# A list schedule at the head of a scan kernel in place of one at its tail

## The chip, the cores and the metric

The kernel runs on one core of a Trainium2 chip. The metric is device time in microseconds (us), the median of several runs. A core has TensorE (PE, matrix products; PEld is its loading of weights), VectorE (DVE), ScalarE (ACT), GpSimd (POOL) and SyncE (SP, which here only issues transfers). Each engine executes its own instructions strictly in the order of the program and waits for the others through semaphores. So the order in which the program emits the work decides what an engine does while it could do something else.

## What is computed

Four images of 64 x 64 pixels with 96 channels go through two layers. Cut to what matters:

```python
x = x + L0(_gn(x))            # _gn: group norm, 32 groups of 3 channels
t = tokens(x)                 # 4 images x 4096 tokens x 96
t = t + attn(_ln_t(t))        # linear attention: no softmax
t = t + ffn(_ln_t(t))         # 96 -> 384 -> 96, products in 8-bit, sums in 16-bit floats

def L0(x):                    # a selective scan over the 4096 tokens
    proj = layernorm(x) @ W_in + b_in
    value, gate, delta = ...  # 96 channels each
    A, B, C = ...             # 96 channels x 16 states each
    h_new = d * (A_t * h) + d * (B_t * u_t)         # token after token
    y = sigmoid(gate) * sum(C_t * h_new, states)
    return y @ W_out + b_out
```

The attention has no softmax. So it is a 97 x 96 matrix R for each image, made from the Gram matrix of all normalised tokens of the image: no token's attention can begin until the last chunk of its image has been scanned.

## The kernel before

An image is cut into 8 chunks of 512 tokens (`TC`), so there are 32 chunks. In each, the 96 x 16 = 1536 channel states are 12 tiles (`NT`) of 128 rows: 4 groups of states (`sh`) times 3 groups of 32 channels (`cg`). One step of the main loop is one tile; there are `K` = 384 steps. A tile is made so:

```python
def b_copy(self):   # ACT: bu <- B product + bias
    nc.scalar.activation(self.bu, self.b_ps, AF.Identity, bias=self.bias(0))
def b_mul(self):    # POOL: times delta*u, replicated over partitions
    nc.gpsimd.tensor_tensor(self.bu, self.bu, rep[self.b, self.i][:, 1, self.cg], ALU.mult)
def a_mul(self):    # DVE: (A product + bias) * delta
    nc.vector.scalar_tensor_tensor(self.a_ps, self.a_ps, self.bias(1),
        rep[self.b, self.i][:, 0, self.cg], ALU.add, ALU.mult)
def scan(self):     # DVE: h[t] = A[t] * h[t-1] + bu[t]
    nc.vector.tensor_tensor_scan(self.h, self.a_ps, self.bu,
        0.0 if self.i == 0 else state[self.sh, self.cg], ALU.mult, ALU.add)
# then C: (C product + bias) * h, on DVE (c_mul) or on ACT and POOL (c_copy, c_mul_pool)
```

Each product is three matrix products (high x high, low x high and so on), since weights and input are split into a high and a low half: `high` rounds the weights on ACT, `low` subtracts on DVE, `split_copies` puts the halves together by DMA. `rep` is delta and delta*u of a chunk, each channel four times over the partitions. For most chunks it goes to DRAM and back (`write`, `read`); for chunk 0:

```python
def copy(self, k, cg, engine):
    t = rep[self.b, self.i][:, k, cg]
    for q in range(4):
        engine.dma_start(t[q * 32 : (q + 1) * 32], self.dd[cg * 32 : (cg + 1) * 32, k])
```

The work ahead of the first scan stands in a fixed order:

```python
for n in range(NCH):                      # group norm of image 0
    q.transpose(n, "AM"[n % 2], "gx"); q.stats(n)
q.aggregate(); q.mean(); q.root(); high_dug(); biases(); q.diagonal(); q.spread(); low_dug()
first, second = Front(0, 0), Front(0, 1)
first.centre(nc.vector); first.scale(nc.vector); first.stats(); first.ln.rstd()
for cg in range(NCG): high(0, cg)         # weights of B, by group of channels
first.apply()
for cg in range(NCG): low(0, cg, nc.vector)
...                                       # A and C likewise, chunk 1 begun
first.proj(2); first.d_out(); first.copy(0, 0, nc.sync)
first.proj(0); first.du_out(); first.copy(1, 0, nc.scalar)
...
```

All other work hangs on steps (`at(step, fn)`): for each chunk a `front` from 22 steps ahead of its scan, a `tail` behind it (sum over states, output product, residual, layer norm, Gram matrix), then `ffn`. The group norm of a later image takes ScalarE's sums of its 8 chunks, each loaded into one buffer (`gx`); image 1 has its own steps:

```python
when = [s0 + SUMS + NT * n for n in range(NCH)]
if b == 1:
    when = [4, 7, 8, 14, 20, 32, 44, 56]
```

What would come behind step K goes into a list instead: each job names its engine, an assumed cost, what it waits for and the buffers it takes, and `Plan.run` emits, time after time, the job that can start first (among near ones that of the lower rank, then that with the longest way to the end). While PE has nothing to do, it runs products whose result nobody uses.

```python
a = job("PE", 0.46, attention, after=[a, b == B - 1 and end.last["r"]], take=[...], free=[...])
a = job("DVE", 0.57, residual, after=[a], free=[f"A:a{nm}"])
a = job("DVE", 1.1, ln.stats, t, after=[a], take=[f"mv:{nm}"])
a = job("POOL", 1.3 if vector else 1.8, ln.rstd, not vector, after=[a])
...
for m in range(NK):
    h = job("PE", 0.24, hidden, m, ...)
    c = job("ACT", 0.57, round_hidden, m, ...)
    r.append(job("DVE", 0.3, relu_vector, m, after=[c]))
a = job("ACT", 1.5, quant, after=r, ...)
a = job("PE", 0.5, project_out, after=[a], ...)
...
end.run(stay_awake)
```

Of the kernel before, what the change touches and what calls it, by code (L numbers as in the profile page):

```python
# [41 lines left out]
XBUFS = 15  # L42


@with_exitstack
def conv_attn_hybrid_kernel(
# [62 lines left out]
    def load_gx(b, i, tag="gx"):  # L109

        t = gxt[b, i] = sb(tag, [P, J, C], F32, f"gx_{b}_{i}")
        nc.sync.dma_start(t, gx_v[b, i])


    for i in range(NCH):
        load_gx(0, i, "x")
# [8 lines left out]
    load_x(0, 0)  # L125
    raw0 = load_raw("cha", 0, A0)
    raws = [load_raw("chb", B0, C * S)]
    load_x(0, 1)
    raws += [load_raw("chb", c0, C * S) for c0 in (A0, C0)]
# [5 lines left out]

    gam = const.tile([C, 1], F32, name="gam")
# [6 lines left out]

    brow = sb("bu", [3 * NCG, 32 * S], F32, "brow")
    for k, c0 in enumerate((B0, A0, C0)):
        nc.scalar.dma_start(
            brow[k * NCG : (k + 1) * NCG, :],
            b_in[c0 : c0 + C * S].rearrange("(g n) -> g n", g=NCG),
        )
# [81 lines left out]
    def split_copies(dst):  # L231
        v = dst.bitcast(F32)
        nc.sync.dma_start(v[0:64, 2], v[0:64, 0])
        nc.sync.dma_start(v[64:P, 2], v[0:64, 1])
# [9 lines left out]
    b_bac = const.tile([P, NSH, 3, NCG], F32, name="b_bac")  # L244

    def cols(k, cg):

        return (
            w_bac[k][:, :, cg].rearrange("k n (s c) -> k n s c", s=S),
            raws[k][:, cg * 32 * S : (cg + 1) * 32 * S].rearrange("k (c s) -> k s c", s=S),  # L250
        )
# [4 lines left out]
    def low_dug():  # L256
        split_low(w_dug, raw0, nc.gpsimd)
        split_copies(w_dug)

    def high(k, cg):  # L260
        dst, src = cols(k, cg)
        nc.scalar.copy(dst[:, 0], src)

    def low(k, cg, engine):
        split_low(*cols(k, cg), engine)
        if cg == NCG - 1:
            split_copies(w_bac[k].rearrange("k n g c -> k n (g c)"))

    def biases():

        row = sb("bu", [3 * NCG, NSH * P], F32, "bias")
        nc.vector.tensor_copy(
            row.rearrange("g (s c) -> g s c", s=S), brow.rearrange("g (c s) -> g s c", s=S)
        )
        ps = bank("M", [P, NSH, 3 * NCG], "bias_ps")
        for sh in range(NSH):
            nc.tensor.transpose(
                ps[:, sh, :], row[:, sh * P : (sh + 1) * P], ident[: 3 * NCG, : 3 * NCG]
            )
        nc.vector.tensor_copy(b_bac.rearrange("p h k g -> p h (k g)"), ps)  # L280
# [29 lines left out]
    class LayerNorm:  # L310
# [13 lines left out]
        def rstd(self, shift=True):  # L324
# [3 lines left out]
            nc.gpsimd.tensor_tensor(self.r, self.r, mhalf, ALU.pow)  # L328
            if not shift:
                return  # L330
            self.nmr = small.tile([P, J], F32, tag="nmr", name=f"nmr_{self.nm}")
            nc.gpsimd.tensor_scalar(self.nmr, self.mv[:, :, 0], -1.0, None, ALU.mult)
            nc.gpsimd.tensor_tensor(self.nmr, self.nmr, self.r, ALU.mult)

# [101 lines left out]
    class GroupNorm:  # L436


        def __init__(self, b):
            self.b = b  # L440
# [9 lines left out]

        def stats(self, n):
            if n == 0:
                self.st = small.tile([C, NCH, 6], F32, tag="gst", name="gst_0", bufs=1)
            nc.vector.bn_stats(self.st[:, n, :], self.ps)
# [49 lines left out]
        def diagonal(self):  # L504
            self.dg = small.tile([C, 2, C], F32, tag="gdg", name=f"gdg_{self.b}", bufs=1)
            for k in range(2):
# [4 lines left out]
        def spread(self):  # L511

            ps = bank("M", [P, 2, C], f"gmr_ps_{self.b}")
            nc.tensor.matmul(
                ps.rearrange("p k c -> p (k c)"), lhsT=ones[0:C, :],
                rhs=self.dg.rearrange("p k c -> p (k c)"), start=True, stop=True,
            )
            t = small.tile([P, 2, C], F32, tag="gmr", name=f"gmr_{self.b}", bufs=2)
            nc.scalar.copy(t, ps)
            gn[self.b] = [t[:, k, :].unsqueeze(1).to_broadcast([P, J, C]) for k in range(2)]  # L520

    def group_norm(b, s0):
# [12 lines left out]
        if b == 1:  # L535
            when = [4, 7, 8, 14, 20, 32, 44, 56]
# [6 lines left out]
        for n, name in ((1, "moments"), (2, "mean"), (4, "root"), (6, "diagonal"), (8, "spread")):  # L543
# [5 lines left out]
    class Front:  # L549
# [3 lines left out]
        def __init__(self, b, i):  # L553
            self.b, self.i, self.nm = b, i, f"{b}_{i}"
            self.ln = LayerNorm(1e-3, f"c_{self.nm}")

# [49 lines left out]
        def copy(self, k, cg, engine):  # L606

            t = rep[self.b, self.i][:, k, cg]
            for q in range(4):
                engine.dma_start(  # L610
                    t[q * 32 : (q + 1) * 32], self.dd[cg * 32 : (cg + 1) * 32, k]
                )
# [18 lines left out]
    def front(b, i, s0, f=None):  # L631
# [10 lines left out]
        at(s + 7, f.transpose)  # L642
        at(s + 8, f.affine)
        at(s + 9, f.upper)
        at(s + 9, f.low)
        at(s + 12, f.proj, 2)
        at(s + 13, f.d_out)
        at(s + 13, f.proj, 0)
        at(s + 14, f.du_out)
        at(s + 14, f.write)  # L650
        at(s + 15, f.read)
# [6 lines left out]
    class Tile:  # L658
# [59 lines left out]
        def slot(self):  # L718
            if self.cg == 0:
# [23 lines left out]
    def state_sum(g, last=None, first=None):  # L743


        if not first:
            y_ps[g] = bank("M" if last is None else "B", [C, TC], f"y_ps_{g}")
        t = chs.pop((g, last or 0))
        for cg in range(NCG):
            nc.tensor.matmul(  # L750
                y_ps[g][cg * 32 : (cg + 1) * 32, :], lhsT=fold, rhs=t[:, cg, :],
                start=not first, stop=(last is None or last == NSH - 1),
                tile_position=(0, 32 * cg), skip_group_check=True,
# [445 lines left out]
```

## Time and profile before

| | us |
|---|---|
| median of 3 runs | 1231.91 (1231.48 to 1232.03) |
| span of the profiled run | 1229.7 |
| first scan starts | 47.00 |
| first scan of the second chunk starts | 90.96 |
| last scan starts | 1152.93 |
| R of the last image done | 1169.2 |
| last GpSimd instruction ends | 1223.4 |

| engine | busy us | share |
|---|---|---|
| PE | 1159.0 | 94% |
| DVE | 1123.9 | 91% |
| POOL | 1028.2 | 84% |
| ACT | 808.4 | 66% |

A timeline line has the start, the duration, the engine, the source line, the operation, output <- inputs, shapes, and in brackets how long the engine had been idle before and what ended that. In a table of stretches the columns are the stretch, its length, the busy time of PE, PEld, DVE, ACT and POOL with counts, the granted TensorE clock (1.00 is full), the share of time in which the DMA engines were busy, and GB/s.

### The profile page before, as it was taken

To read this page: it belongs to the slowest core of one execution; us is meant where nothing else is said; L and a number is where in the kernel's file an instruction comes from. 1 tells how busy PE (TensorE), PEld (TensorE's weight loads), DVE (VectorE), ACT (ScalarE), POOL (GpSimd) and SP (SyncE) were. 2 spreads that over 40 slices of the span, in tenths; PEclk is the share of its full clock that TensorE was granted. 3 is DMA by queue.
4 is the path that set the end of the run, shared out by engine and by line. 5 is a ranking of instruction groups with operands and counts; after the bars stand their busy time and mean duration, and the time that the engine had idled before them with its cause. 6 is when DMAs were issued, how large, how long until landed. Compare 5 with 4: busy or idle time off the path is not lost. (4 is left out here: it accounts for less than half of the span.)

```text
span 1229.7 us, 19138 instructions
## 1 busy us (share of the span) xinstructions
PE 1159.0 (94%) x5866; PEld 872.1 (71%) x5866; DVE 1123.9 (91%) x2095; ACT 808.4 (66%) x1806; POOL 1028.2 (84%) x1168
## 2 busy tenths in 40 slices
PE   3689999999999999999999999999999999999985
PEld 2467777677777777677777777677777777777663
DVE  5479999999999999899999999899999999999884
ACT  3455555555555677677877777777677677777474
POOL 4367888888888888999999889899999899989654
PEclk7789999999999999999999999999999999999999
DMA  8566776677778767777777677677777676767221
GB/s 197 134 136 139 171 163 154 141 155 165 155 172 174 157 149 158 162 154 160 165 175 157 149 169 174 134 155 159 171 156 153 153 173 151 154 149 162 60 70 39
DMA packets 102116, 185.20 MB, mean 151 GB/s; under 512 B 42865, under 2 KB 47413, under 8 KB 102014
## 3 DMA queue, kind: packets, MB, share of 16 engines
q1 hardware_dynamic: 87708, 109.78, 38.0%
q0 software_dynamic: 13536, 73.93, 30.3%
q8 instruction: 46, 0.75, 0.3%
q10 hardware_dynamic: 770, 0.28, 0.1%
q14 instruction: 56, 0.46, 0.1%
HBM read 70.69 MB, written 24.77 MB: 78 GB/s over the span
## 5 line engine op out<-in xcount | busy, mean ns | idle before, releaser
L686 POOL TENSOR_TENSOR bu<-bu,rep 128x512 f32<-128x512 f32 x384 | 559.3, 1504 | 32.9 <-DMA rep<-dd 21.1
L683 ACT ACTIVATE bu<-Bps,b_bac 128x512 f32<-128x512 f32 x384 | 264.2, 688 | 288.2 <-PE Bps L240 275.5
L702 DVE TENSOR_TENSOR_SCAN h<-Aps,state,bu 128x512 f32<-128x512 f32 x336 | 426.4, 1269 | 12.5 <-POOL bu L686 3.5
L695 DVE SCALAR_TENSOR_TENSOR Aps<-Aps,b_bac,rep 128x512 f32<-128x512 f32 x384 | 282.3, 735 | 41.2 <-PE Aps L240 32.8
L240 PE MATMUL Bps<-xs,w 128*128 128x512 f32 x768 | 269.6, 432 | 4.9 <-ACT bu L683 4.8
L240 PE MATMUL Aps<-xs,w 128*128 128x512 f32 x768 | 250.6, 407 | 11.8 <-DVE h L702 10.6
L735 POOL TENSOR_TENSOR ch<-ch,h 128x512 f32<-128x512 f32 x128 | 194.4, 1519 | 2.5 <-ACT ch L732 2.3
L240 PEld LDWEIGHTS Aps<-xs,w 128*128 128x128 f32 x768 | 139.5, 190 | 70.3 <-DVE h L702 41.6
L240 PEld LDWEIGHTS Bps<-xs,w 128*128 128x128 f32 x768 | 130.7, 192 | 46.5 <-issue 26.0
L240 PE MATMUL Bps<-xl,w 128*128 128x512 f32 x384 | 153.1, 399 | 0.0
L240 PE MATMUL Aps<-xl,w 128*128 128x512 f32 x384 | 153.0, 399 | 0.0
L240 PE MATMUL Dps<-xs,w 128*128 128x512 f32 x384 | 121.5, 398 | 0.0
L240 PE MATMUL Cps<-xs,w 128*128 128x512 f32 x384 | 121.0, 396 | 0.0
L741 POOL DMA_DIRECT2D ch<-ch x94 | 88.5, 941 | 20.1 <-DMA ch<-ch 16.5
L726 DVE SCALAR_TENSOR_TENSOR ch<-Dps,b_bac,h 128x512 f32<-128x512 f32 x128 | 94.7, 740 | 0.6 <-PE Dps L240 0.5
L726 DVE SCALAR_TENSOR_TENSOR ch<-Cps,b_bac,h 128x512 f32<-128x512 f32 x128 | 95.0, 742 | 0.0
L240 PEld LDWEIGHTS Bps<-xl,w 128*128 128x128 f32 x384 | 73.0, 190 | 17.3
L240 PEld LDWEIGHTS Dps<-xs,w 128*128 128x128 f32 x384 | 72.6, 189 | 17.9
L240 PEld LDWEIGHTS Cps<-xs,w 128*128 128x128 f32 x384 | 72.2, 188 | 17.9
L240 PEld LDWEIGHTS Aps<-xl,w 128*128 128x128 f32 x384 | 72.4, 189 | 16.9
L240 PE MATMUL Dps<-xl,w 128*128 128x512 f32 x192 | 76.1, 396 | 0.0
L240 PE MATMUL Cps<-xl,w 128*128 128x512 f32 x192 | 75.9, 395 | 0.0
(176 smaller groups left out, 2045.6 us busy)
## 6 DMA issues: line engine op xcount, KB each, us to landing
ch<-ch POOLq DMA_DIRECT2D x94, 768.0 KB, 6.8
rep<-ddd SPq DMA_DIRECT2D x124, 384.0 KB, 7.0
ddd<-dd SPq DMA_DIRECT2D x31, 384.0 KB, 3.1
xl<-lo SPq DMA_DIRECT2D x64, 128.0 KB, 2.9
gx<-in_x_dram SPq DMA_DIRECT2D x32, 192.0 KB, 3.3
x<-in_x_dram SPq DMA_DIRECT2D x32, 192.0 KB, 3.0
xatd<-xat SPq DMA_DIRECT2D x32, 192.0 KB, 3.2
xal<-xatd SPq DMA_DIRECT2D x32, 192.0 KB, 3.9
```

The costliest lines, as they stand in the source:

```text
L240: nc.tensor.matmul(ps, lhsT=wt[:, n], rhs=mv, start=(n == 0), stop=(n == 2))
L683: nc.scalar.activation(self.bu, self.b_ps, AF.Identity, bias=self.bias(0))
L686: nc.gpsimd.tensor_tensor(self.bu, self.bu, rep[self.b, self.i][:, 1, self.cg], ALU.mult)
L695: nc.vector.scalar_tensor_tensor(self.a_ps, self.a_ps, self.bias(1), rep[self.b, self.i][:, 0, self.cg], ALU.add, ALU.mult,)
L702: nc.vector.tensor_tensor_scan(self.h, self.a_ps, self.bu, 0.0 if self.i == 0 else state[self.sh, self.cg], ALU.mult, ALU.add,)
L726: nc.vector.scalar_tensor_tensor(self.slot(), self.c_ps, self.bias(2), self.h, ALU.add, ALU.mult)
L735: nc.gpsimd.tensor_tensor(self.ch, self.ch, self.h, ALU.mult)
L741: nc.gpsimd.dma_start(chs[g, 0], chs.pop((g, sh)), accum_op=ALU.add)
```

## The change

The list schedule moves from the end to the beginning. Up to the sixth step (`START = 6`) all work is emitted by `Plan.run`; behind the last scan the work returns to fixed steps. Four things go with it:

1. Chunk 0 goes without transfers between engines: the low half of its input is subtracted straight into place, and delta and delta*u come already replicated out of TensorE, through weights that hold each column four times (`w_rep`).
2. The weights are split by group of states, in 12 pieces, so that the first steps need only the first pieces.
3. Image 0 is loaded once; its group norm reads the same tiles as the scan path.
4. The sums of image 1's group norm lie seven steps apart.

```diff
     for i in range(NCH):
-        load_gx(0, i, "x")
+        load_x(0, i)
+        gxt[0, i] = xt[0, i]
...
+    def repeat(n):
+        for k, c0 in enumerate((2 * C, 0)):
+            for cg in range(NCG):
+                c = c0 + cg * 32
+                nc.gpsimd.tensor_copy(
+                    w_rep[:, n, k * NCG + cg].rearrange("p (q c) -> p q c", q=4),
+                    w_dug[:, n, c : c + 32].unsqueeze(1).to_broadcast([P, 4, 32]),
+                )
...
-            when = [4, 7, 8, 14, 20, 32, 44, 56]
+            when = [8, 15, 22, 29, 36, 43, 50, 57]
...
-        def copy(self, k, cg, engine):
...
+        def low_in_place(self, n):
...
+            dst, c0, c1 = ((xs[C:P], 64, C), (xl[0:64], 0, 64), (xl[64:P], 0, 64))[n]
+            nc.vector.tensor_tensor(dst, self.ps[c0:c1], xs[c0:c1].bitcast(F32), ALU.subtract)
+        def wide(self, k, cg):
+            ps = self.wd[k, cg] = bank("M", [P, TC], f"wide{k}{cg}_ps")
+            project(ps, w_rep[:, :, k * NCG + cg], split[self.b, self.i])
...
-            end.last["gram"] = job("DVE", 0.25, gram_sum, after=[a], free=[f"B:g{i}"])
...
+        at(s0 + 21, gram)
+        at(s0 + 22, gram_out)
         if i:
+            at(s0 + 23, gram_add)
...
+        if drain:
+            plan = [
+                (-2, fetch), (0, attention), (1, residual), (2, ln.stats, t), (3, ln.rstd),
+                (4, apply), (5, transpose), (5, quant_in),
+                (6, hidden, 0), (6, hidden, 1), (6, hidden, 2),
+                (7, relu, 0), (7, relu, 1), (7, relu, 2), (8, quant),
+                (9, project_out), (9, round_out), (10, bias_out), (11, total), (11, store),
+            ]
...
+    def planned_start():
...
+        hd = job("ACT", 0.43, high_dug, after=[land("raw", 11.9)])
+        ld = job("POOL", 0.8, low_dug, after=[hd])
+        wr = [job("POOL", 2.2, repeat, n, after=[ld]) for n in range(2)]
...
+        a = job("DVE", 0.56, first.scale, nc.vector, after=[c, *g])
+        a = job("DVE", 1.1, first.stats, after=[a])
+        a = job("DVE", 0.07, first.ln.offset, after=[a])
+        a = job("POOL", 1.05, first.ln.root, after=[a])
+        a = job("DVE", 1.3, lambda: first.ln.apply_vector(first.t, first.t), after=[a])
...
+        plan.run(stay_awake)
...
-    end.run(stay_awake)
```

The plan under `drain` is that of the last image, whose chunk i begins at step K + 27 + 2i. With the schedule at the end go its details: the last chunk's sums over states in three parts as the groups come (group 1 added to group 0 by DMA, then 0, 2 and 3 by products; now 1 and 2 are added by DMA first), the last chunk's normalisation on VectorE without the shift, rounding of the output in turn on ACT and DVE (now always DVE for the last image), ReLU by DVE for the chunks of image 2 that are left (now ACT), and the unused products that fill PE. New filler products (128 x 128) stand in the planned start.

## The prediction

> **What bounds the kernel now.** I read the busy shares by slice first, then the busy time of stretches, then the timeline of VectorE around the first scans and behind the last one.
>
> ```profile
> DVE  5479999999999999899999999899999999999884
> PEclk7789999999999999999999999999999999999999
> ```
>
> From the fourth slice (30.7 us each) to the 37th VectorE is full; that middle is 384 steps of one scan each, and the change leaves its work alone. What it touches are the two ends. The busy time of stretches (columns: PE, PEld, DVE, ACT, POOL, clock, DMA share, GB/s) sizes them:
>
> ```profile
> 0.00:47.00 47.00, 21.84 (x75) 15.21 (x76) 21.39 (x48) 20.28 (x33) 16.29 (x37) 0.67 0.76 175
> 47.00:90.96 43.96, 35.68 (x141) 26.48 (x140) 30.02 (x44) 20.85 (x51) 28.15 (x26) 0.88 0.62 139
> 1154.20:1169.20 15.00, 14.07 (x101) 9.70 (x99) 9.69 (x44) 6.28 (x12) 6.55 (x12) 1.00 0.23 67
> 1169.20:1209.00 39.80, 34.28 (x250) 24.02 (x248) 35.64 (x129) 30.09 (x48) 23.54 (x30) 1.00 0.21 61
> ```
>
> Up to the first scan (47.0) no engine is busy half the time: that is latency. The first twelve steps (47.0 to 90.96, chunk 0) leave VectorE idle for 13.9 of 44 us. Behind the last scan (1154.2) it takes 15.0 us until the attention matrix R stands, then VectorE is 90% busy until 1209. Which waits open the start, from the timeline:
>
> ```profile
> 35.61 2.44 SPq L610 DMA_DIRECT2D rep<-dd  x4
> ...
> 40.52 1.27 POOL L686 TENSOR_TENSOR bu<-bu,rep 128x512 f32<-128x512 f32 x1 [10.02 <-DMA rep<-dd]
> ...
> 47.00 1.21 DVE L702 TENSOR_TENSOR_SCAN h<-Aps,bu 128x512 f32<-128x512 f32 x1
> ...
> 55.49 1.22 DVE L702 TENSOR_TENSOR_SCAN h<-Aps,bu 128x512 f32<-128x512 f32 x1 [3.17 <-POOL bu L686]
> ...
> 79.26 1.09 PE L446 MATMUL gx_ps<-ident,gx 128*96 128x128 f32 x4 [4.76 <-DMA gx<-in_x_dram]
> ...
> 90.96 1.27 DVE L702 TENSOR_TENSOR_SCAN h<-Aps,state,bu 128x512 f32<-128x512 f32 x1
> ```
>
> The 24 small copies that spread delta over the partitions hold GpSimd for 10 us, then again before the third scan. At 79 TensorE, in order, stands behind image 1's third load of group-norm input (one buffer; the sums come at steps 4, 7, 8): the tenth scan starts at 75.89, the eleventh at 84.89. And the end:
>
> ```profile
> 1152.93 1.28 DVE L702 TENSOR_TENSOR_SCAN h<-Aps,state,bu 128x512 f32<-128x512 f32 x1
> ...
> 1168.97 0.26 DVE L885 COPY rmat<-r_ps 97x96 f32<-97x96 f32 x1 [0.50 <-PE r_ps L870]
> ...
> 1222.44 0.91 POOL L990 TENSOR_TENSOR o<-x,yb 128x384 f32<-128x384 f32 x1
> ```
>
> **What the Trainium skill says.** (1) "TensorE: Matmul & The Clock Gate", Part 1, What's actually happening: the PE clock runs at half rate after some 3.4 us of idling and at full rate after about as long busy. The trace agrees: granted clock 0.50 from 14 to 32 us, a pair of products 1.22 us at 40.35 against 0.63 at 47.5. (2) "SBUF — State Buffer", Who interferes with whom: a VectorE operation with two SBUF inputs, or in a two-port mode, and a GpSimd operation lock each other out. It agrees: the root on GpSimd takes 1.66 us at 19.7 beside VectorE's weight subtraction, 1.04 alone. (3) "DMA: Bandwidth & Descriptors", Anatomy of one DMA: some 2 us of fixed cost per transfer; the 64 KB copies of delta take 2.0 us to landing. (4) The same page, Specifications: pieces under 512 B don't reach line rate. The x loads (384 B pieces) that now serve group norm 0 too took 3.3 us, the 1536 B loads 3.6: no penalty seen, so I charge none.
>
> **The change, start.** Removed: two of ten x loads (2 x 0.4 us of issue ahead of the weights), 24 copies, and the hop of the low half over DMA. Added: twelve GpSimd copies for repeated weights, six products with ScalarE and VectorE evictions, three VectorE subtractions. Moved: the weight halves in twelve pieces by state group. I follow the longest path in the order in which the changed program issues; durations are those of the trace.
> - Mean and root of group norm as before: second diagonal done at 15.0; spread 0.5 and copy 0.25: 15.8. Centring was done meanwhile; scale 0.56, stats and aggregates 1.1: **17.6**.
> - The root stands on GpSimd behind the low half of w_dug (0.79 after 14.6), twelve copies of 128x128 (estimate 0.4 each, between 0.25 for 128x32 and 1.27 for 128x512) and chunk 1's centring (1.0): it starts near 21.2, and with up to 1.66 is done at **22.6**. Here 3.5 us go lost that the list doesn't see.
> - Apply 1.3, transposes 0.6, affine 0.74, upper 0.58, three subtractions of 0.69, hops: **28.1**.
> - ScalarE, in order, still makes four C weight pieces (0.8 each, from 1.058 for 512 columns) until 29.3; then d 0.69, B 0.69, d 0.69. VectorE: two du (0.74), then a multiply 0.73, scan at **33.5**, against 47.0.
> - Scans 0 to 5 are VectorE's then: 6 x 1.21 + 6 x 0.73 + 4 x 0.74 + du, du, lo, stats (0.74 + 0.74 + 0.69 + 1.1) = 17.9: scan 6 at 51.4, against 69.03.
> - Five steps at 2.35 (69.03 to 75.89 is three at 2.29): scan 11 at 63.2, and 3.9 more (87.10 to 90.96 before) to scan 12: **67**. Chunk 1's replicated delta: lo at 43, 2.9 of transfers, two products with evictions until 49, 3.1 to write, 7 to read: 60, just in time for the multiply ahead of scan 12. The load that cost 9 us at 76 is gone, since the sums lie seven steps apart.
> Against 90.96 that is 24; I count 1 back for locks: **-23 us**. Of these about 13.5 stand at the first scan, 4 more at the seventh, 6 from the group norm.
>
> **The change, end.** The list schedule behind the last scan goes; fixed steps in program order come back, without filler products.
> - R: before, 15.0 us. Now ScalarE has, in order, between the last scan and the copy of the last Gram matrix: six hidden groups of three passes (0.58 + 0.72 + 0.63 = 1.93 each, 11.6), four applies of 1.54, two quantisations 0.6, two keeps 0.57, two roundings 0.48, two Gram copies 0.24: 21.5 us from 1152.5. The last chunk's apply waits besides for a sum that needs the third state group's gather (a GpSimd DMA of 7 us) and GpSimd's root with shift (0.23 + 1.04 + 0.24 + 0.20): some 4 us more. 1178, adding 0.4, four small products with copies 3.3 as before: **1182** against 1169.2, **+12.5**.
> - From R on, before, 60.5 us. Now eight chunks on VectorE: residual 0.54, stats 1.1, apply 4 x 0.48, relu 3 x 0.55, rounding 0.55 = 5.7, less 0.4 of overlap: 8 x 5.3 = 42.5; lead-in 4, holes of the last chunk 5, GpSimd's two adds 1.9, last store to the end 6.3 (1223.35 to 1229.7): 60. **0**; chunk 7 of image 2 lies earlier now, which pays for the roundings.
> End: **+12**. Sum: 1231.9 - 23 + 12 = **1221 us**.
>
> **Rivals.** (a) The start bounds itself by other waits: weights in twelve pairs of transfers behind each other in one queue. For it: the DMA is 99% busy until 25 us. Against: A's first piece is asked for at 25 to 26 and needed at 30. It would leave scan 0 at 38 and make 1226. (b) Chunk 1's delta comes late and stalls scan 12 by 4: 1225. (c) The end is as good in order as by list, since VectorE bounds both (90% busy): end +5, 1214. Against it: R hangs on ScalarE's order. (d) TensorE goes cold in the end without fillers: it is busy 34 of 40 us now, fillers included; at half rate attention, transposes, hidden and output products (3.1 us a chunk, warm) need about 6 and take over as the bound: +6, 1227. (e) The list holds as its author meant it, root not late: scan 0 at 30, 1217.
>
> **Range and chances.** Start between -17 and -28, end between +6 and +17; the extremes together are rare, so 1210 to 1233 for 8 in 10. 2% below 1231.9 is 1207.3: that needs a start of -28 and an end of +4, 8%. Above 1256.5 nothing leads: 1%.
>
> **What the profile of the changed kernel would show.** First scan at 33.5, seventh at 51, thirteenth (the first with a state) at 67; no wait of TensorE for gx near scan 9; GpSimd's root at 21 behind the copies. Middle steps as long as before: from scan 12 to the last scan 1062 us. R 28 us behind the last scan; end 88 behind it (75.5 before). Wrong it would be if the middle changed length, if scan 12 came later than 75, or if the order behind the last scan cost nothing.

## The result, and the profile after

The changed kernel takes 1245.07 us (median of 4 runs, 1242.68 to 1246.44), the kernel before, run beside it, 1231.7 us (4 runs, 1230.77 to 1232.03). The ratio is 1.0108, 95% interval 1.0088 to 1.0127. So it is 1.1% slower; 1221 us was predicted, with a range of 1210 to 1233. The span of the profiled run is 1244.6 us, against 1229.7 before.

The same two rows of the page as before, 40 slices of now 31.1 us each:

```profile
DVE  6869999999999999899999999999999999999274
PEclk8989999999999999999999999999999999999655
```

The middle is full as before. At the end VectorE falls to 20% in a slice of its own (the 2), and the granted clock of TensorE, 0.9 to the very end before, is 0.6, 0.5, 0.5 in the last three slices. The stretches, cut at the first scan, scan 12, the end of the last scan, R and on (columns as before: stretch, length, busy time of PE, PEld, DVE, ACT and POOL, clock, DMA share, GB/s):

```profile
0.00:39.56 39.56, 29.85 (x158) 25.84 (x159) 26.70 (x54) 17.49 (x29) 24.82 (x52) 0.83 0.69 168
39.56:85.60 46.04, 35.65 (x150) 26.96 (x149) 31.23 (x44) 21.47 (x49) 28.47 (x26) 0.89 0.52 114
85.60:1150.20 1064.60, 1044.01 (x5243) 790.63 (x5241) 1021.23 (x1824) 725.47 (x1663) 949.23 (x1058) 1.00 0.70 156
1150.20:1181.80 31.60, 20.85 (x106) 12.32 (x105) 7.16 (x33) 21.14 (x43) 9.42 (x18) 0.64 0.24 66
1181.80:1223.00 41.20, 34.97 (x187) 27.28 (x186) 31.57 (x128) 25.72 (x39) 23.97 (x43) 0.54 0.19 53
```

The first scan comes 7.4 us earlier (39.56 against 47.00), but the first twelve steps take 46.0 us instead of 44.0, so at scan 12 only 5.4 of it are left. The middle takes 1064.6 instead of 1063.2. R takes 31.6 us from the end of the last scan instead of 15.0, and no engine is busy for much more than two thirds of them. That gives the 15 us between the two spans: 5.4 gained up to scan 12, 1.4 lost in the middle, 18.9 lost behind the last scan (95.7 us from its start to the end of the span, against 76.8).

Three waits of the start, from the timeline of all engines:

```profile
13.64 5.04 PE L1166 MATMUL awake<-ident 128*128 128x128 f32 x22
18.48 0.58 PE L553 MATMUL gmr_ps<-gdg,ones 96*128 96x96 f32 x2
20.43 0.77 DVE L606 TENSOR_TENSOR z<-z,gmr 128x384 f32<-128x384 f32 x1 [0.33 <-ACT gmr L562]
...
22.54 1.54 POOL L367 TENSOR_TENSOR rstd_c<-rstd_c,mhalf 128x4 f32<-128x4 f32 x1 [1.75 <-DVE rstd_c L364]
24.03 2.35 POOL L235 TENSOR_TENSOR w<-raw,w 128x384 fp32r<-128x384 f32 x2
24.11 4.42 DVE L378 TENSOR_SCALAR z<-z,mv_c,rstd_c 128x96 f32<-128x96 f32 x4 [0.17 <-POOL rstd_c L367]
...
58.70 2.04 SPq L687 DMA_DIRECT2D rep<-ddd  x4
60.78 0.44 SPq L113 DMA_DIRECT2D gx<-in_x_dram  x1
69.72 1.09 PE L480 MATMUL gc_ps<-ident,gx 128*96 128x128 f32 x4 [9.69 <-DMA gx<-in_x_dram]
75.03 1.21 DVE L766 TENSOR_TENSOR_SCAN h<-Aps,bu 128x512 f32<-128x512 f32 x1
```

First, eleven of the new unused products (22 passes) stand in TensorE's queue ahead of the first spread of the group norm, whose input was ready at 13.2. Second, the apply of chunk 0 takes 4.42 us (24.11 to 28.53), while GpSimd runs three weight subtractions and chunk 1's scaling one after the other (24.03 to 28.46). Third, and largest: at 60 TensorE stands for 9.7 us behind the first load of image 1's group norm. That load is issued only at 60.78, behind the four reads of chunk 1's delta in the same queue, and beside them it takes 8.9 us to land. Scan 7 starts at 60.47 and scan 8 at 75.03. The stall of the kernel before, at 79, was not removed but moved forward, and it is longer.

The way to R and to the end:

```profile
1153.99 1.99 PE L938 MATMUL a_ps<-rmat,xal 97*128 97x96 f32 x8 [2.83 <-DMA xal<-xatd]
1156.63 3.20 PE L815 MATMUL y_ps<-ch,fold 128*32 128x512 f32 x12 [0.22 <-DVE x L943]
1159.90 0.69 DVE L830 TENSOR_TENSOR yg<-y_ps,gate 96x512 f32<-96x512 f32 x1 [2.26 <-PE y_ps L815]
1165.47 1.54 ACT L371 ACTIVATE xa<-x,nmr_a,rstd_a 128x96 f32<-128x96 f32 x4 [1.95 <-POOL nmr_a L359]
1173.99 0.98 PE L988 MATMUL y_ps<-w_q,hq 128*128 128x96 fp8e5 x10 [1.93 <-ACT hq L979]
1174.77 1.59 PE L858 MATMUL gram_ps<-xa 128*97 128x97 f32 x8
1181.56 0.26 DVE L918 COPY rmat<-r_ps 97x96 f32<-97x96 f32 x1 [0.73 <-PE r_ps L899]
1237.28 0.91 POOL L1008 TENSOR_TENSOR o<-x,yb 128x384 f32<-128x384 f32 x1
```

The gated sum (`yg`) starts 11.0 us behind the start of the last scan (1148.92), before it was 5.0. The sums over states (`y_ps<-ch,fold`) that it needs stand in TensorE's order behind the attention of a chunk of image 2 (`a_ps`), and TensorE waits 2.83 us for that one's input. The third group's transfer is not what they wait for: issued at 1146.55, it takes 5.8 us to land, so it is there at 1152.4, 4.3 us before they start. The input of the last Gram product is complete at 1167.0, but the product starts at 1174.77: in the fixed order it stands behind an output product of image 2, which waits for ScalarE.

### The profile page after: what moved, and what is told of

It reads as the page before. It is cut to its first block, busy times and chain, and to the rows that moved or that the text cites. A ratio compares the mean times of both kernels' runs of the same rounds, so it can differ in the third digit from the quotient of the medians.

```text
span 1244.6 us, 19222 instructions
## 1 busy us (share of the span) xinstructions
PE 1171.2 (94%) x5881; PEld 886.9 (71%) x5881; DVE 1124.8 (90%) x2090; ACT 818.1 (66%) x1827; POOL 1043.2 (84%) x1204
## 5 line engine op out<-in xcount | busy, mean ns | idle before, releaser
L766 DVE TENSOR_TENSOR_SCAN h<-Aps,state,bu 128x512 f32<-128x512 f32 x336 | 426.4, 1269 | 13.2 <-POOL bu L750 3.5
L245 PEld LDWEIGHTS Aps<-xs,w 128*128 128x128 f32 x768 | 138.2, 188 | 68.1 <-DVE h L766 40.1
L245 PEld LDWEIGHTS Bps<-xl,w 128*128 128x128 f32 x384 | 72.5, 189 | 17.6
L245 PEld LDWEIGHTS Dps<-xs,w 128*128 128x128 f32 x384 | 72.4, 188 | 17.6
L245 PEld LDWEIGHTS Aps<-xl,w 128*128 128x128 f32 x384 | 72.2, 188 | 17.6
```

The costliest lines, as they stand in the source:

```text
L245: nc.tensor.matmul(ps, lhsT=wt[:, n], rhs=mv, start=(n == 0), stop=(n == 2))
L766: nc.vector.tensor_tensor_scan(self.h, self.a_ps, self.bu, 0.0 if self.i == 0 else state[self.sh, self.cg], ALU.mult, ALU.add,)
```

## The experiments

All times of stages are from the profiled runs. "R" is the start of the copy `rmat`, counted from the start of the last scan; "rest" runs from there to the end of the span.

| kernel | first scan | scan 12 | last scan | R | rest | median us | ratio to before (95%) |
|---|---|---|---|---|---|---|---|
| before | 47.00 | 90.96 | 1152.93 | 16.0 | 60.8 | 1231.7 | 1 |
| changed | 39.56 | 85.60 | 1148.92 | 32.6 | 63.1 | 1245.07 | 1.0108 (1.0088 to 1.0127) |
| e1_gx_first | 38.02 | 72.69 | 1136.01 | 33.2 | 62.1 | 1235.11 | 1.0028 (1.0016 to 1.0039) |
| e2_no_start_fill | 40.85 | 86.92 | 1148.54 | 31.8 | 63.1 | 1242.61 | 1.0087 (1.0070 to 1.0104) |
| e3_drain_fill | 39.65 | 85.62 | 1148.10 | 39.3 | 58.6 | 1247.87 | 1.0132 (1.0117 to 1.0147) |
| e4_old_end | 39.11 | 85.24 | 1148.50 | 16.0 | 61.0 | 1227.42 | 0.9970 (0.9958 to 0.9982) |
| e5_before_spacing | 45.96 | 83.09 | 1147.66 | 16.0 | 60.9 | 1225.78 | 0.9953 (0.9938 to 0.9968) |
| e6_gram_early | 37.62 | 82.87 | 1145.97 | 27.8 | 64.5 | 1240.23 | 1.0077 (1.0062 to 1.0092) |
| e7_start_two | 35.08 | 69.43 | 1132.36 | 33.2 | 61.9 | 1228.62 | 0.9977 (0.9970 to 0.9984) |
| e8_start_three | 35.30 | 68.70 | 1131.01 | 32.9 | 60.8 | 1227.26 | 0.9971 (0.9960 to 0.9983) |
| e9_both_lists | 34.90 | 69.24 | 1132.88 | 16.0 | 61.2 | 1212.09 | 0.9842 (0.9827 to 0.9857) |
| e10_both_hold | 33.27 | 68.12 | 1131.32 | 16.0 | 60.8 | 1210.34 | 0.9829 (0.9813 to 0.9845) |
| e11_fill_behind_r | 40.10 | 85.60 | 1151.37 | 27.9 | 60.9 | 1240.96 | 1.0071 (1.0050 to 1.0092) |
| e12_one_gather | 39.95 | 85.84 | 1149.62 | 25.0 | 62.9 | 1238.99 | 1.0073 (1.0049 to 1.0097) |
| e13_three_end | 38.65 | 84.19 | 1146.67 | 24.1 | 60.8 | 1237.10 | 1.0051 (1.0033 to 1.0068) |
| e14_relu_vector | 39.12 | 85.30 | 1150.14 | 28.6 | 61.6 | 1237.91 | 1.0055 (1.0037 to 1.0073) |
| e15_warm_all | 39.16 | 85.05 | 1149.47 | 25.3 | 58.3 | 1233.83 | 1.0030 (1.0020 to 1.0041) |
| e16_warm_relu | 38.48 | 84.31 | 1147.24 | 25.9 | 60.0 | 1236.72 | 1.0046 (1.0032 to 1.0061) |

Ten of these kernels (the changed one, e3, e4, e6 and e11 to e16) have the same start, and their first scan lies between 37.62 and 40.10. So a difference of less than 2.5 us at the first scan between two single profiles says nothing, and where a stage is compared I take differences within one profile. Five kernels share the changed end (the changed one, e1, e2, e7, e8): their R lies between 31.8 and 33.2, their rest between 60.8 and 63.1. The middle, from scan 12 to the last scan, lies between 1061.6 and 1065.8 over all kernels of the table. The median of e10_both_hold counts one slow run of 1941.99 us, at a granted clock of 0.65; its other three lie between 1209.79 and 1210.81, and the ratio rests on these.

### Which part moved the time: the start

**e1_gx_first.**

```diff
-        at(when[0] - 7, load_gx, b, 0)
+        if b != 1:
+            at(when[0] - 7, load_gx, b, 0)
...
+        job("SP", 0.4, load_gx, 1, 0, after=[b])
         a = job("SP", 0.5, second.write, after=[a], late=3.4)
```

> Changed kernel, but image 1's first group-norm load is issued ahead of the write and the four reads of chunk 1's delta instead of behind them. Theory (the in-order transfer queue holds that load back, TensorE stands 9.7 us behind it, and every later engine with it): the wait of the transposes at 69.7 us falls under 1 us, scan 8 starts at 63 to 66 instead of 75.03, scan 12 at 75 to 78 instead of 85.6, time down by 8 to 10 us to 1235 to 1237. Rival (chunk 1's replicated delta, which lands near 67, is the next wait at once): scan 8 moves as said, but scan 12 only to 79 to 82, time down by 4 to 6. Rival (the load is hidden anyway, something else holds TensorE at 60): no change.

```profile
58.34 0.60 PE L480 MATMUL gc_ps<-ident,gx 128*96 128x128 f32 x4
...
72.69 1.27 DVE L767 TENSOR_TENSOR_SCAN h<-Aps,state,bu 128x512 f32<-128x512 f32 x1
```

The wait is gone (no bracket behind the transposes; the load, issued at 48.98, landed 2.9 us later), scan 12 comes 34.7 us behind the first scan instead of 46.0, and the time falls by 10.0 us. Chunk 1's delta is no new wait: scan 11 starts at 68.83 and scan 12 3.9 us later, the same 3.9 as before (87.10 to 90.96). The first theory holds; scan 12 came even earlier than it said.

**e5_before_spacing** asks what the spacing alone is worth, in the kernel before.

```diff
-            when = [4, 7, 8, 14, 20, 32, 44, 56]
+            when = [8, 15, 22, 29, 36, 43, 50, 57]
```

> The kernel before with one line changed: image 1's group-norm sums at steps 8, 15, 22, 29, 36, 43, 50, 57 instead of 4, 7, 8, 14, 20, 32, 44, 56. Theory (the spacing is worth what I charged for it, as long as the first load stands ahead of the reads of chunk 1's delta in the transfer queue, which it does here): TensorE's wait of 4.8 us at 79 goes, scan 12 at 82 to 84 instead of 90.96, time down by 7 to 9 us to 1223 to 1225. Rival (in any order some load of the group norm meets the reads of delta, so the stall only moves): time within 2 us of the kernel before.

Scan 12 at 83.09, 7.9 us earlier (6.8 of them between the first scan and scan 12), and the time falls by 0.47% (0.32 to 0.62), that is 5.8 us (3.9 to 7.6), less than the 7 to 9 that I expected. The last scan comes 5.3 us earlier: the stretch from scan 12 to the last scan is 1064.6 here and 1062.0 before, both within the range of all kernels. The same line gains in one kernel and stalls in the other. What differs is the place of the first load in the queue: here it is issued at step 1, ahead of the reads of delta at step 5; in the changed kernel everything up to the sixth step, these reads included, is emitted by the list, and the load follows.

**e2_no_start_fill** takes the unused products out of the start.

```diff
-        plan.run(stay_awake)
+        plan.run()
```

> Changed kernel without the unused 128 x 128 products in the planned start. Theory (eleven of them stand in TensorE's queue ahead of the first spread and delay it by 5 us, and the next 28 delay the wide products a little): first spread at 13.4 to 14 instead of 18.5, scale at 17 instead of 20.4, first scan at 35.5 to 37 instead of 39.56, time down by 2 to 4 us. Rival (they earn their place: without them TensorE stays at half rate and the wide products and the first steps take twice as long): first spread early as said, but the first scan at 38 to 41 and the time the same or up to 2 us longer, since the stall behind the group-norm load at 60 us takes up what is gained (then scan 8 starts at 73 to 75 in either case).

The first spread runs early, but the second does not:

```profile
13.75 0.44 PE L553 MATMUL gmr_ps<-gdg,ones 96*128 96x96 f32 x2
14.55 5.17 DVE L292 COPY bias<-brow 6x128 f32<-6x128 f32 x1
15.78 2.90 POOL L271 CAST w_rep<-w_dug 128x128 fp32r<-128x128 f32 x12
19.97 0.74 PE L553 MATMUL gmr_ps<-gdg,ones 96*128 96x96 f32 x2
```

A copy of 6 x 128 elements took 5.17 us on VectorE, as long as GpSimd copied w_rep and centred chunk 1 beside it (in the changed kernel it took 1.37 and was done as these copies began). The transposes of the bias rows wait for it, and the second spread stands behind them. So taking away the unused products alone gains nothing at the first scan: the wait behind them was covered by another of the same length. The time is 0.2% lower, within the two intervals.

**e7_start_two** is e1_gx_first with both taken away:

```diff
     def bias_rows():
-        nc.vector.tensor_copy(
+        nc.scalar.copy(
...
-            if hasattr(tiles[1], "c_ps"):
+            if not hasattr(first.ln, "mv") or hasattr(tiles[1], "c_ps"):
```

> The kernel with the early group-norm load (e1_gx_first), and two more edits in the start: the bias rows are copied by ScalarE instead of VectorE, and the unused products begin only after chunk 0's statistics. Theory (the first spread was held by eleven unused products; without them it was held by a 6 x 128 copy on VectorE that took 5.17 us beside GpSimd's twelve copies; with both gone nothing stands ahead of it): spreads at 13.5 to 16, scale at 16.5 to 17.2 instead of 20.4, root still behind GpSimd's copies and chunk 1's centring at 19 to 20, apply done at 25 to 26.5 instead of 28.5, first scan at 35 to 36.5 instead of 38.0, time 2 to 3 us under e1_gx_first. Rival (the two-port lock moves on: the centring, scale or apply on VectorE then meets GpSimd's twelve copies and grows): first scan 37 to 38, time the same as e1_gx_first.

First scan at 35.08, against 38.02 in the profile of e1_gx_first and 37.62 to 40.10 in the others; scale at 16.16, the root at 19.24. The median is 6.5 us below that of e1_gx_first, more than the 2 to 3 that I expected; the spans of the two profiles differ by 3.8 us only, 2.9 of them at the first scan. ScalarE, which waited for the spread too, now begins with the weights at 15.1 instead of 19.1 in e1_gx_first; whether that is the part that I had not counted was not tested.

**e8_start_three** places GpSimd's low halves of the third and fourth group behind the apply in the list:

```diff
+        for t in held:
+            t["after"].append(a)
```

> As e7_start_two, and GpSimd's low halves of the third and fourth group of states wait for chunk 0's apply. Theory (the apply took 4.42 us instead of 1.1 to 1.3 because two subtractions on GpSimd ran beside it): apply 1.1 to 1.4 us, first scan 2.5 to 3.5 us earlier than in e7_start_two, time 2 to 3.5 us less. Rival (the subtractions only move to where they lock VectorE's other weight subtractions, or make the third group's weights late): apply short, but the first scan at most 1 us earlier or scan 6 no earlier than in e7_start_two, time within 1 us of it.

```profile
20.61 4.43 DVE L378 TENSOR_SCALAR z<-z,mv_c,rstd_c 128x96 f32<-128x96 f32 x4 [0.17 <-POOL rstd_c L367]
21.48 3.48 POOL L235 TENSOR_TENSOR w<-raw,w 128x384 fp32r<-128x384 f32 x3
```

The apply was as long as ever, so this run tested nothing of the lock. The list only decides the order in which instructions are emitted; between engines nothing made GpSimd wait, and it ran the subtractions at once.

**e10_both_hold** (with the old end, see below) makes GpSimd wait by data: a copy of one column of the normalised input stands ahead of them.

```diff
+        hold = job("POOL", 0.1, lambda: nc.gpsimd.tensor_copy(warm, first.t[:, J - 1, 0:1]), after=[a])
+        for t in held:
+            t["after"].append(hold)
...
-        a = job("POOL", 1.0, second.scale, nc.gpsimd, after=[a])
+        a = job("POOL", 1.0, second.scale, nc.gpsimd, after=[a, hold])
```

> As e9_both_lists, and GpSimd copies one column of chunk 0's normalised input ahead of chunk 1's scaling and of the low halves of the third and fourth group, so that these really wait for the apply (in e8_start_three the list only placed them behind it, and GpSimd ran them beside it all the same: apply 4.43 us). Theory (two-port lock): apply 1.0 to 1.4 us, first scan 2 to 3.3 us earlier than in e9_both_lists, time 1 to 3 us less. Rival (the lock moves to VectorE's two weight subtractions behind it, and chunk 1's delta comes later): apply short, first scan at most 1 us earlier or scan 12 no earlier, time the same or longer.

The apply in e9_both_lists, then in e10_both_hold:

```profile
20.55 4.44 DVE L380 TENSOR_SCALAR z<-z,mv_c,rstd_c 128x96 f32<-128x96 f32 x4
```

```profile
20.56 1.05 DVE L380 TENSOR_SCALAR z<-z,mv_c,rstd_c 128x96 f32<-128x96 f32 x4
```

What GpSimd's work beside it costs the apply is shown: 3.4 us. The first scan comes only 1.6 us earlier and scan 12 only 1.1; that is less than single profiles can tell apart, though e7_start_two, e8_start_three and e9_both_lists, with the long apply, lie close together (34.90 to 35.30). In this profile GpSimd, later now with the weights, makes the first scan wait 1.75 us for its multiply. So the apply is as the theory said, and the first scan lies between what theory and rival said. The time is 0.13% lower and the intervals overlap.

### Which part moved the time: the end

**e4_old_end**: the new start, with the whole list schedule of the kernel before behind the last scan.

> New start with the end of the kernel before (list schedule behind the last scan, with its unused products); group-norm load as in the changed kernel. Theory (start and end are two separate terms): from the last scan to the end 76 to 77 us as before, instead of 95.7; last scan at 1149; time 1226 to 1228, 4 us under the kernel before. Rival (some of the end's loss comes from the start's or middle's changed phase): 1230 or more.

R 16.0 and rest 61.0, as in the kernel before; 17.7 us under the changed kernel. The end's loss is the end's own.

**e3_drain_fill**: unused products in the fixed end.

```diff
+        if s >= K:
+            if s == K:
+                warm_ps = bank("D", [P, TC], "warm_ps")
+            for _ in range(4):
+                nc.tensor.matmul(
+                    warm_ps, lhsT=w_dug[:, 0, 0:P], rhs=w_bac[0][:, 0, 0], start=True, stop=True
+                )
```

> Changed kernel with four unused 128 x 512 products behind every step from the last scan's step on (none during the scans). Theory (TensorE is granted 0.5 to 0.64 behind the last scan, and heads the chain there): clock at 0.9 or more to the end, sums of the last chunk 1.9 instead of 3.2 us, attention 1.0 instead of 2.0, R 28 to 30 us behind the last scan instead of 32.9, R to the end 57 to 59 instead of 62.8: time down by 6 to 9 us. Rival (the order on ScalarE and the latency of one chunk bound the end, TensorE's half rate is hidden): clock up, but the time within 2 us of the changed kernel's. Rival (the unused products get in the way of the needed ones, in order): time up by 2 to 5.

```profile
PEclk8989999999999999999999999999999999999999
```

The clock is full to the end, and the rest falls from 63.1 to 58.6. But R comes at 39.3 instead of 32.6: four products a step, in order, stand in the way of those that are needed. The third expectation is what happened: 6.7 us lost ahead of R, 4.5 gained behind it. The time goes up by 2.8, but the two intervals overlap.

**e6_gram_early** moves the last Gram product, what follows from it and the chunks behind R seven steps forward:

```diff
-        at(s0 + 21, gram)
+        n = s0 - 7 if s0 == K else s0
+        at(n + 21, gram)
...
-            at(s0 + 24 + n, fn)
+            at(s0 + (17 if s0 == K else 24) + n, fn)
...
-                s = K + 27 + DRAIN_EVERY * i
+                s = K + 20 + DRAIN_EVERY * i
```

> Changed kernel with the last chunk's Gram matrix, its copy and sum, the four products for R and the chunks behind R seven steps earlier in the fixed order; nothing else. Theory (R waits because TensorE, in order, takes the Gram product only behind the output product of image 2's last chunk, 7.8 us after its input is ready): R 24 to 26 us behind the last scan's start instead of 32.9, time down by 6 to 8 us to 1237 to 1239. Rival (ScalarE's 21 us of work between the last scan and the Gram copy set R, wherever the product stands): R moves by 2 us at most and so does the time. Rival (R comes early but image 2's last chunk is then in the way of the chunks behind R): R early, time down by 2 to 4.

R at 27.8 instead of 32.6: 4.8 us, short of the 7 to 9 that I expected. The rest is 1.4 above the longest of the five kernels with the changed end; why was not tested. The time falls by 4.8 us, where I expected 6 to 8. That the Gram product's place holds R is shown.

**e12_one_gather**: e6_gram_early, and besides only the second group of states of the last chunk is added by transfer.

```diff
-                if g < N - 1 or sh < NSH - 1:
+                if g < N - 1 or sh == 1:
```

> As e6_gram_early, but of the last chunk only the second group of states is added by transfer, the third goes into the product as in the kernel before. Theory (the sum over states waits 6 us longer than in the kernel before, for the third group's gather): the gated product starts 6 to 8 us behind the last scan's start instead of 11.3, R at 23 to 25 instead of 27.8, time down by 3 to 4. Rival (TensorE stands in order behind the transfer of image 2's next input and takes the sums after that in any case): the gated product moves by 1 us at most, time within 1 us.

```profile
1151.82 1.13 PE L940 MATMUL a_ps<-rmat,xal 97*128 97x96 f32 x8
```

The gated sum starts 8.5 us behind the last scan instead of 11.3, R at 25.0 instead of 27.8. The timed medians don't tell the two kernels apart (1238.99 and 1240.23). The size is near what the theory said, but the trace points to the rival's mechanism: in e6_gram_early, as in the changed kernel, TensorE waits 2.83 us for the input of image 2's attention (`xal`), which takes 4.9 us to land; here `xal` is issued 1.0 us earlier, counted from the last scan, and lands in 2.5, and the wait is gone. Every kernel with both transfers and a fixed end, unless unused products stand ahead of R, shows this wait (2.81 to 2.84 us), and none with one does. So the transfer that was left out held up another one, and not the sum that reads its result.

**e11_fill_behind_r**: e6_gram_early with three unused products behind each step, but only once R stands (`s >= K + 24`).

> As e6_gram_early, with three unused 128 x 512 products behind every step from the first that has R (none before it). Theory (behind R TensorE at half rate is the bound; the harm of the unused products in e3_drain_fill came ahead of R, where they stood in the way): clock near 1.0 from R on, R unchanged at 27 to 28 behind the last scan, R to the end 58 to 60 instead of 64.5, time 4 to 6 us under e6_gram_early. Rival (VectorE and ScalarE in their fixed order bound that stretch, TensorE's half rate is hidden): R to the end 63 or more, time within 1.5 us.

R unchanged (27.9), the rest 60.9 instead of 64.5: 3.6 us, at a granted clock of 0.86 instead of 0.58 in the 41 us behind R. The timed median doesn't show it (1240.96 against 1240.23; the intervals overlap). In the profile, the first scan is 2.5 us later and the last one 5.4. From the last scan's start to the end it is 88.8 us against 92.3.

**e13_three_end** has the three edits together.

> Changed kernel with three edits in the end together: Gram matrix and what hangs on it seven steps earlier (e6_gram_early), of the last chunk only the second group by transfer (e12_one_gather), three unused products behind every step from R on (e11_fill_behind_r). Theory (three separate causes, each with its own part of the way): R 24.5 to 25.5 us behind the last scan's start, R to the end 59 to 61.5, so 84 to 87 us from the last scan's start to the end, against 95.7 in the changed kernel and 76.8 in the one before; time 1232 to 1236. Rival (the three lie beside each other, the longest covers the rest): 88 us or more, as with one of them.

84.8 us from the last scan to the end, of 95.7 in the changed kernel: the three nearly add up. The median, 1237.10, is above the 1232 to 1236 that I expected. Of the 18.9 us lost, 8.0 are left, and all of them lie ahead of R (24.1 against 16.0).

**e14_relu_vector** tests the cause that the prediction named, ScalarE's order:

```diff
-            if drain:
+            if drain or late:
...
+            if late:
+                plan.insert(14, (14, quant))
```

(`late`: image 2, chunks 6 and 7.)

> As e13_three_end, and for the last two chunks of every image but the last two images' rest nothing else: image 2's chunks 6 and 7 take their ReLU on VectorE and one quantisation, as in the kernel before, which takes five passes a chunk off ScalarE (about 2.6 us each chunk) behind the last scan. Theory (what is left of R's delay is ScalarE's order, as the prediction had it): R at 20 to 22.5 us behind the last scan's start instead of 24.5 to 25.5, time down by 2.5 to 4. Rival (what is left is latency from engine to engine in a fixed order, with ScalarE idle a third of that time): R moves by 1.5 us at most, time within 1.5 us of e13_three_end.

R came later, 28.6, but TensorE's clock differed. The sums over states in e13_three_end, then in e14_relu_vector:

```profile
1150.94 2.77 PE L815 MATMUL y_ps<-ch,fold 128*32 128x512 f32 x18
```

```profile
1155.10 5.01 PE L815 MATMUL y_ps<-ch,fold 128*32 128x512 f32 x18
```

As a test of ScalarE this settles nothing. So both were run again with one unused product behind every step ahead of R: **e15_warm_all** and **e16_warm_relu**.

```diff
-        if s >= K + 24:
+        if s >= K:
...
-            for _ in range(3):
+            for _ in range(3 if s >= K + 24 else 1):
```

> As e13_three_end, with one unused 128 x 512 product also behind every step between the last scan and R (three behind every step from R on, as there). Theory (what is left of R's delay is TensorE at half rate: sums over states 2.8 to 5.0 us instead of some 1.6, attention 1.6 to 2.0 instead of 1.1, Gram 1.5 instead of 0.85, small products 0.6 instead of 0.4): the sums take 1.6 to 2.8, R 20 to 22.5 us behind the last scan's start instead of 24.1 to 28.6, time 2 to 4 us under e13_three_end. Rival (what is left is the chain from engine to engine in its fixed order, and unused products in the order cost what the clock gives): R at 24 or more.

> As e15_warm_all, with the ReLU of image 2's chunks 6 and 7 on VectorE as in e14_relu_vector, whose reading a half-rate TensorE disturbed (the same 18 products took 5.01 us there and 2.77 in e13_three_end). Theory (ScalarE's order holds R): R 2.5 us or more earlier than in e15_warm_all. Rival (it does not): R within 1 us of e15_warm_all.

R of e15_warm_all (last scan at 1149.47), then of e16_warm_relu (last scan at 1147.24):

```profile
1174.81 0.26 DVE L920 COPY rmat<-r_ps 97x96 f32<-97x96 f32 x1 [0.50 <-PE r_ps L901]
```

```profile
1173.17 0.26 DVE L920 COPY rmat<-r_ps 97x96 f32<-97x96 f32 x1 [0.73 <-PE r_ps L901]
```

25.3 and 25.9, with sums over states of 2.77 and 2.78 us: as the rivals said, neither edit brings R forward. But neither run clears what it was to test. The first unused product in e15_warm_all has to wait:

```profile
1151.66 0.50 PE L1240 MATMUL warm_ps<-w,w_dug 128*128 128x512 f32 x1 [2.58 <-DVE ch L790]
```

It writes the bank that VectorE's multiply for the last tile still reads, and everything behind it in TensorE's order waits too: the sums over states start 7.3 us behind the start of the last scan, against 4.3 in e13_three_end. From the start of the last Gram product to R it then takes 7.7 us instead of 9.2. So what the clock gave there, the unused products had taken before, and what R would be at full clock without that wait was not measured. The median is 3.3 us below that of e13_three_end, with intervals that overlap; the rest is 2.5 us shorter.

In e16_warm_relu the last Gram product starts 1.4 us earlier than in e15_warm_all, but from there to R it takes 9.7 us. The third of R's four products stands behind an output product of image 2, in e15_warm_all and then in e16_warm_relu:

```profile
1173.21 0.60 PE L990 MATMUL y_ps<-w_q,hq 128*128 128x96 fp8e5 x10 [0.97 <-ACT hq L981]
```

```profile
1171.15 0.68 PE L991 MATMUL y_ps<-w_q,hq 128*128 128x96 fp8e5 x12 [2.60 <-ACT hq L985]
```

ScalarE's one quantisation of 1.48 us, which waits for the last ReLU, makes TensorE wait longer than the last of the three short ones (2.64 us in e14_relu_vector). So the edit took passes off ScalarE and put a longer wait for ScalarE in R's way; it doesn't show that ScalarE's order has no part. What keeps R at 24 to 26 us in a fixed order, where the list reaches 16, stays open between the clock, ScalarE and the order itself. What the trace of e13_three_end shows is where: of the 8.0 us, 5.0 lie between the start of the last Gram product and R (9.2 against 4.2 before), where work of image 2 stands between R's four products on TensorE and between their copies on VectorE.

### Both lists

**e9_both_lists**: the start of e7_start_two and the end of the kernel before.

> The start of e7_start_two (early group-norm load, bias rows on ScalarE, unused products only after chunk 0's statistics) with the end of the kernel before (list schedule). Theory (start and end are separate terms): scan 12 at 69 to 70, 76 us from the last scan to the end, 1210 to 1213. Rival (the earlier start meets transfers that lengthen the middle, or the end depends on the phase): 1215 or more.

1212.09 us: as the first theory said, start and end are separate terms. With the hold of e10_both_hold, 1210.34, ratio 0.983 (0.981 to 0.985). Both beat the kernel before and the changed one.

## Why the prediction was wrong, step by step

**"The load that cost 9 us at 76 is gone, since the sums lie seven steps apart": this step failed, and it is the largest.** I looked at the distance between the sums and not at what stands ahead of the first load in its queue. The stretch from the first scan to scan 12 was to take 33.5 us (33.5 to 67) and took 46.0; e1_gx_first, which moves nothing but that load, brings it to 34.7. That is 11.4 of the 18.6 us by which scan 12 missed its 67. The spacing itself is worth 6.8 us there when the first load goes out early (e5_before_spacing).

**Scale and stats at 17.6, "second diagonal done at 15.0; spread 0.5": failed.** Scale ended at 21.2 and the aggregates at 22.3. The unused products in the start were in the diff and I left them out of the path. Their removal alone shows nothing, because the 6 x 128 copy, another item that I gave no time, takes just as long. e7_start_two removes both.

**The root "stands on GpSimd behind" twelve copies of 0.4 each and starts at 21.2: wrong in its cause.** The copies took 2.92 us together, 0.24 each, and GpSimd then waited 1.75 us for VectorE. It ended at 24.1 because its input was late. (The sum had a slip besides: 21.2 and 1.66 make 22.9, not 22.6.)

**"Apply 1.3": failed, 4.42.** The prediction quoted "SBUF — State Buffer", section Who interferes with whom, for the root, and didn't apply it to the next step. The section says that a VectorE operation in a two-port mode and GpSimd lock each other out. e9_both_lists and e10_both_hold agree: 4.44 us beside GpSimd's work, 1.05 without. The four operations of the apply come through about one to each of GpSimd's operations (1.0 to 1.2 us each); in which mode they run, no run here shows.

**Scans 0 to 5 in 17.9 us: near** (18.97). **Chunk 1's delta "just in time": right in that nothing waits for it** (e1_gx_first). So with the two waits in e7_start_two's start taken out, and the lock in e10_both_hold, the first scan comes at 33.27 and scan 12 at 68.1, where the prediction had 33.5 and 67. The sum was that of a kernel without those waits. That it fits so well is partly luck: in e10_both_hold the apply ends at 21.6, 2.3 us ahead of the predicted 23.9 (22.6 and 1.3), and the way from there to the first scan takes 11.7 us where the prediction had 9.6.

**Middle unchanged: right within 1.4 us** (1063.3 against 1062.0 from scan 12 to the last scan).

**R +12.5: right that it is late; the path to it failed.** It is +16.6. "ScalarE has 21.5 us in order" is true as a count (21.1 us busy), but R is not the sum of these passes: ScalarE is idle for a third of the stretch. R waits where TensorE, in order, stands for a single pass or transfer ahead of what R needs. Two such places are shown. The last Gram product stands behind an output product that waits for ScalarE (moved forward: 4.8 us). The sums over states stand behind an attention that waits for its input (2.8 us with the third group's transfer gone). The second I had within "some 4 us more", as a wait of the sum for that transfer itself, which had landed 4.3 us before. The 8.0 us that are left stay open.

**R to the end "0": wrong by up to the 2.3 us of rival (d).** The five kernels with the changed end take 60.8 to 63.1, those with the list 60.8 to 61.2. TensorE at half rate is what the prediction had put under "TensorE: Matmul & The Clock Gate", section What's actually happening, and then left to a rival at 6 us. The trace agrees that it matters here, at a smaller size: with a granted clock of 0.93 or more in the 41 us behind R (e3_drain_fill, e15_warm_all, e16_warm_relu) the rest is 58.3 to 60.0, at 0.54 (the changed kernel) and 0.58 (e6_gram_early) it is 63.1 and 64.5. So the clock was missing in the sum. (8 x 5.3 in it is 42.4, not 42.5.)

The rivals: (a), the weights' transfers, and (b), the late delta, were not seen. (c), an end as good in order, is refuted by e4_old_end, (e), scan 0 at 30, by every run. (d) is part of the answer. Together: predicted -23 and +12; measured -4.0 at the last scan and +18.9 behind it.

## What to carry to other kernels

When loads are spread out over time, look first at what stands ahead of the first one in its queue: a transfer that waits for an engine holds back every later one (here the load issued only at 60.78), and an engine that takes its work in order then stands behind a load that could have been made long before. Every filler, copy and small setup item in a start that is bound by latency belongs on the path that one follows by hand, since nothing there hides behind a full engine, and one item of 5 us is as long as the gain. A list that orders instructions doesn't make engines wait: in this kernel only data between the two engines kept them apart (e8_start_three against e10_both_hold).

## What I had not expected of the hardware

A copy of 6 x 128 elements on VectorE lasted 5.17 us beside back-to-back copies on GpSimd (e2_no_start_fill), while four applies beside GpSimd's longer subtractions came through in turn, one for each. The prediction quoted some 3.4 us of idling ahead of half rate; in the changed kernel the granted clock falls to 0.50 at 1152.43, 3.5 us behind the start of the last scan, although TensorE was busy for 1.83 of these 3.5 us and had then been idle for only 1.3. Whether it falls ahead of the sums over states differs between profiles: 18 passes took 2.77 us in one and 5.01 in another kernel with the same products there. And ten profiles of one and the same start differ by 2.5 us at the first scan; where that comes from is open.
